# An attention and layer-norm kernel on one core: the last pairs' order written anew, and GpSimd's closing multiply and add of two tiles set apart

## The chip, the cores and the metric

The kernel runs on one core of a Trainium2 chip. TensorE (PE) multiplies, with its weight loads (PEld) beside it; VectorE (DVE), ScalarE (ACT) and GpSimd (POOL) work on tiles of 128 partitions; SyncE (SP) only issues transfers. ScalarE and GpSimd issue some transfers too. Each engine takes its instructions in the order in which they are written, and waits on semaphores where an input is not there yet. The metric is the time of one execution in microseconds (us), here the median of some runs.

## The reference

Cross-attention of 4 x 2048 rows of x (512 wide, 16 heads of 32) to 77 rows of context, a mask on the context, an output product, the residual and a layer norm with a scale and a shift:

```python
qs = (q @ wq).reshape(Bq, Lq, H, HD).transpose(0, 2, 1, 3)
ks_ = (k @ wk)...; vs = (v @ wv)...
scores = jnp.einsum('bhqd,bhkd->bhqk', qs, ks_) / jnp.sqrt(jnp.float32(HD))
scores = jnp.where(mask[:, None, :, :], -jnp.inf, scores)
attn_w = jax.nn.softmax(scores, axis=-1)
attn = jnp.einsum('bhqk,bhkd->bhqd', attn_w, vs)
out = attn.transpose(0, 2, 1, 3).reshape(Bq, Lq, H * HD) @ wo + q
mu = jnp.mean(out, axis=-1, keepdims=True)
var = jnp.mean((out - mu) ** 2, axis=-1, keepdims=True)
return (out - mu) / jnp.sqrt(var + EPS) * gamma + beta
```

All is float32. gamma and beta are drawn, not ones and zeros.

## The kernel before

The 8192 rows are 64 tiles of 128 (t = 0 to 63), two tiles make a pair (b = 0 to 31), four a group (16 groups). A float32 product is done as three products of parts: each operand is split into a high part and a low rest, and high x high, high x low and low x high are added up.

No loop and no planner sets the order. A string, ORDER, lists some 2,100 words, one for each step, in the order in which they are written to the engines; a table at the end of the kernel maps the first letter to a function. The number is a tile, pair or group, the figure behind the point a quarter or a part. The words of the stretch that changes, by engine:

- TensorE: Q60 (one quarter of a group's queries, 12 products), S58 (a tile's scores, 64 small products), V26 (a pair's weights times values, 32), O48 (a tile's output product, 12), X62 (x itself as the first product of an output). W62 and W63 are V for single tiles of the last pair.
- VectorE: q (queries out of PSUM), T58.2 (mask and maxima of four heads), r (reciprocal of the sums), t (transpose of the weights), b and d (the low part of V's and W's result), + and $ (the residual, into SBUF or kept in PSUM), s (mean and variance), y and z (subtract the mean and multiply by gamma; multiply by the inverse root and add beta), >63.0 and >63.1 (z for tile 63 in halves), h (r for a half tile).
- ScalarE: e58.2 (exponentials of four heads), a and c (the high part of V's and W's result), i (high part of x), k and % (scale and shift of a tile), = (mean and variance of tiles 60 and 62 there).
- GpSimd: n and m (the weights times the reciprocals), j (low part of x), v and u (inverse roots for a pair, for one tile), @ (u and the shift), f (times gamma, plus beta: two operations on 128 x 512).
- Transfers: x (a tile of x in), w and < (a result out, < in halves) from SyncE, the last half from ScalarE; P26.4s (part 4 of 12 of pair 26's regrouped weights, from SyncE; a: from ScalarE, g: from GpSimd), U62.5g the same for a single tile of the last pair; g (x transposed, for the queries).

So a tile ends in one of two ways: by s, u, y, z on VectorE, or by s, @ or v, % or k, and f on GpSimd; then w stores it. V reads what all 12 P of its pair have brought; t needs n, n needs r, r needs four e, and each e its T.

Two tables go with ORDER. SLOTS gives, for each buffer, the slot that it takes in the order of allocation; "mm" are the eight banks of PSUM, and whoever takes a bank waits until its last holder has been read. PADS gives for each Q and O (in base 36) how many empty instructions stand between its 12 products.

The functions of this change and of the prediction: rsqrt_one (L640, inverse root), shift_one (L648), centre and finish (L656, L661, L664 for the halves), stats_act (L634), affine (L619 to L622), store and store_half (L624, L670), regroup_part (L487, transfers at L493), o_proj (L568, products at L579), av_tile (W, products at L522).

Of the kernel before, what the change touches and what calls it, by code (L numbers as in the profile page):

```python
# [131 lines left out]
P28.10g x55 P28.2g x61 S61 P28.4g e60.1 +53 P28.6g O51 r59 T60.3 n59 k47 T61.2 e60.3 T61.0 T61.3 f47 S62 T61.1
e60.0 t59 V27 e61.1 r60 T62.2 e61.3 P29.11s P29.0g T62.3 O52 P29.7g x50 s51 P29.4g P29.8s a27.0 T62.0 P29.3g a27.1
P29.2s s53 P29.6g e61.0 w45 P29.1g V28 b27.0 P29.10s n60 y51 e61.2 x62 b27.1 T62.1 O55 a28.0 r61 @53 a28.1 $50
e62.3 +52 n61 b28.1 b28.0 k46 S63 t60 e62.2 x54 f46 O54 e62.1 t61 P29.5a +55 w46 e62.0 T63.1 X63 P30.11g P29.9s
T63.0 P30.5g O57 P30.6s P30.3g T63.2 e63.1 P30.1s u51 r62 s52 P30.0s n62 e63.2 s50 P30.2s P30.8s X62 T63.3 e63.3
P30.10s s55 V29 u50 w47 y50 e63.0 @52 z51 @55 z50 w51 O56 a29.0 h63.0 P30.4a $57 m63.0 h63.1 a29.1 b29.0 P30.9a s57
m63.1 P30.7a b29.1 O58 %55 u57 t62 %53 f55 %52 $56 U62.2s U62.11a V30 $54 U62.1s U62.10a +58 U62.6s U62.3a f53 t63
U62.4a O59 a30.0 a30.1 s58 U63.4s U63.1a U63.11s b30.0 @58 U62.8a U62.9s b30.1 U62.0a s56 U62.7s O61 U63.9a U62.5g
# [39 lines left out]
def xattn_layernorm(  # L179
# [410 lines left out]
    def residual_psum(t):  # L590
        nc.vector.tensor_tensor(pos[t], pos[t], od[t], ALU.add)
# [27 lines left out]
    def affine(t):  # L619
        o = od[t]  # L620
        nc.gpsimd.tensor_tensor(o, o, gam, ALU.mult)  # L621
        nc.gpsimd.tensor_tensor(o, o, bet, ALU.add)  # L622
# [11 lines left out]
    def stats_act(t):  # L634
        mv = mvs[t, 1] = tiny.tile([P, 4], F32, tag="mvt", bufs=64 - LATE, name=f"mvt_{t}")
        nc.scalar.activation(od[t], pos[t], AF.Copy, scale=-1.0 / D, accum_out=mv[:, 3:4])
        nc.scalar.activation(od[t], pos[t], AF.Square, bias=mv[:, 3:4], accum_out=mv[:, 1:2])
# [196 lines left out]
```

## Time and profile before

| | us |
|---|---|
| median of 3 runs (lowest, highest) | 510.38 (510.31, 512.49) |
| the profiled execution's own time | 509.93 |
| its span | 508.1 |
| TensorE busy | 497.6 |
| VectorE busy | 471.3 |
| ScalarE busy | 465.6 |
| GpSimd busy | 420.0 |

The profile is of one execution. Its times count from the start of the span. A row of the timeline has the start, the length, the engine, the line and what is written and read, and in brackets how long the engine stood idle before it and for whom. "x4" means four instructions in a row. Lengths overlap a little at their ends, since an engine begins the next while it drains the last; the step from start to start is then the better measure.

### The profile page before, as it was taken

The page shows a single profiled execution, that of the slowest core. Times are in us where ns is not written, and L with a number is a line of the kernel's source. Part 1 is how long each engine was busy: PE and PEld are TensorE (multiplying, and loading weights), DVE is VectorE, ACT ScalarE, POOL GpSimd, SP SyncE. Part 2 cuts the span into 40 slices and gives each one's busy share as a digit, 9 for nine tenths or more (in the row PEclk, how much of TensorE's full clock was granted, in tenths as well). Part 3 has the DMA queues.
Part 4 walks back from the last instruction along what each step waited for, and adds up shares of the span by engine and source line. Part 5 has one row for each costly group of instructions (what it writes and reads, how often), then busy time and mean ns, then how long its engine had stood idle before and what let it go on. Part 6 is the DMA issues. An engine that isn't in the chain of part 4 may idle for free.

```text
span 508.1 us, 21810 instructions
## 1 busy us (share of the span) xinstructions
PE 497.6 (98%) x6834; PEld 384.0 (76%) x6834; DVE 471.3 (93%) x2565; ACT 465.6 (92%) x2228; POOL 420.0 (83%) x388
## 2 busy tenths in 40 slices
PE   8999999999999999999999999999999999999994
PEld 6987777777777777777777877777787777776663
DVE  5798999999999999999999999999999999999986
ACT  6699999998999999999999999999999999999622
POOL 2573756999978998989899898888989679999986
PEclk9999999999999999999999999999999999999999
DMA  8947767878987687796877678777777687777755
GB/s 298 397 154 215 177 185 171 239 195 237 261 239 220 192 243 198 204 261 189 237 205 239 198 218 229 213 226 211 225 207 219 182 225 214 209 210 198 213 153 228
DMA packets 59236, 110.96 MB, mean 218 GB/s; under 512 B 9430, under 2 KB 12270, under 8 KB 59126
## 3 DMA queue, kind: packets, MB, share of 16 engines
q1 hardware_dynamic: 54854, 101.63, 69.1%
q0 software_dynamic: 2624, 6.16, 4.4%
q10 hardware_dynamic: 1648, 1.77, 1.4%
q8 instruction: 60, 0.98, 0.9%
q14 instruction: 50, 0.41, 0.3%
HBM read 41.79 MB, written 16.78 MB: 115 GB/s over the span
## 4 chain that ended last, share of the span: by engine, by line
PE 85%; DVE 5%; DMA 4%; POOL 3%; SPq 2%; issue 1%; ACTq 0%; ACT 0%; DVEq 0%
PE pq L290 33%; PE po L579 28%; PE sc L414 10%; PE pa L507 10%; PE pv L341 2%; DVE pbuf L431 1%; DVE B L482 1%; PE pk L313 1%; DMA xtl<-x 1%; DMA PT<-B 1%; SPq L493 1%; DMA first_xth<-xw 1%; POOL mvt L646 1%; PE pq L724 1%; DVE q L304 0%
## 5 line engine op out<-in xcount | busy, mean ns | idle before, releaser
L446 ACT ACTIVATE pbuf<-pbuf,nm 128x77 f32<-128x77 f32 x1024 | 352.4, 350 | 3.6 <-DVE nm L431 3.4
L446 ACT ACTIVATION_READ_ACCUMULATOR pbuf<-pbuf,nm 128x1 f32 x1024 | 195.3, 191 | 0.0
L431 DVE CUSTOM_DVE_ANT_0 pbuf<-sc,mb 128x77 f32<-128x77 f32 x1024 | 170.8, 232 | 6.8 <-PE sc L414 3.6
L461 POOL TENSOR_TENSOR pbuf<-pbuf,ri 128x1232 f32<-128x1232 f32 x63 | 142.8, 2268 | 29.1 <-DVE ri L456 27.6
L579 PE MATMUL po<-woh,AH 128*128 128x512 f32 x256 | 102.1, 399 | 0.4 <-DVE nm L431 0.4
L290 PE MATMUL pq<-xth,wqh 128*128 128x512 f32 (+1 forms) x256 | 101.2, 395 | 0.3
L579 PE MATMUL po<-woh,AL 128*128 128x512 f32 x256 | 99.8, 390 | 0.8 <-DVE AL L540 0.8
L579 PE MATMUL po<-wol,AH 128*128 128x512 f32 x256 | 99.7, 390 | 0.0
L290 PE MATMUL pq<-xth,wql 128*128 128x512 f32 (+1 forms) x256 | 98.1, 383 | 0.0
L290 PE MATMUL pq<-xtl,wqh 128*128 128x512 f32 (+1 forms) x256 | 98.1, 383 | 0.0
L482 DVE STREAM_TRANSPOSE B<-pbuf 128x1280 f32<-128x1280 f32 x64 | 96.1, 1501 | 0.9 <-POOL pbuf L461 0.2
L431 DVE DVE_READ_ACCUMULATOR2_ANT nm<- 128x1 f32 x1024 | 83.8, 82 | 0.0
L273 POOL TENSOR_TENSOR xtl<-xtf,xth 128x1024 fp32r<-128x1024 f32 x28 | 67.3, 2406 | 4.3 <-ACT xth L269 4.3
L622 POOL TENSOR_TENSOR o<-o,bet 128x512 f32<-128x512 f32 x51 | 66.0, 1294 | 4.0
L414 PEld LDWEIGHTS sc<-kct,q 32*64 32x64 f32 x4096 | 51.2, 130 | 22.2 <-issue 11.0
L621 POOL TENSOR_TENSOR o<-o,gam 128x512 f32<-128x512 f32 x51 | 67.0, 1314 | 0.2 <-issue 0.2
L414 PE MATMUL sc<-kct,q 32*64 32x77 f32 x4096 | 60.6, 238 | 0.0
L507 PE MATMUL pa<-PT,vsb 96*32 96x256 f32 x992 | 59.7, 382 | 0.0
L579 PEld LDWEIGHTS po<-woh,AH 128*128 128x128 f32 x256 | 48.0, 188 | 13.9 <-issue 1.7
L290 PEld LDWEIGHTS pq<-xth,wqh 128*128 128x128 f32 x256 | 48.1, 188 | 12.3 <-issue 1.2
L579 PEld LDWEIGHTS po<-woh,AL 128*128 128x128 f32 x256 | 48.1, 188 | 11.6 <-DVE AL L540 1.5
L290 PEld LDWEIGHTS pq<-xth,wql 128*128 128x128 f32 x256 | 48.1, 188 | 9.7
(127 smaller groups left out, 641.9 us busy)
## 6 DMA issues: line engine op xcount, KB each, us to landing
PT<-B SPq DMA_DIRECT2D x337, 128.0 KB
xtf<-xT SPq DMA_DIRECT2D x28, 512.0 KB
o<-x SPq DMA_DIRECT2D x56, 256.0 KB
out<-o SPq DMA_DIRECT2D x56, 256.0 KB
PT<-B POOLq DMA_DIRECT2D x29, 128.0 KB, 3.9
stage_a<-wk SPq DMA_DIRECT2D x4, 256.0 KB
stage_b<-wo SPq DMA_DIRECT2D x4, 256.0 KB
stage_a<-xT SPq DMA_DIRECT2D x2, 512.0 KB
```

The lines of the kernel that those rows point to most:

```text
L273: nc.gpsimd.tensor_tensor(l[:, c : c + 2], fx.pop((g, c)), xh[g][:, c : c + 2].bitcast(F32), ALU.subtract)
L290: nc.tensor.matmul(pq, w[:, c, m * P : (m + 1) * P], r[g][:, c, rs], start=(n == 0), stop=(n == 11))
L341: nc.tensor.matmul(pv[: rows.stop - rows.start], ctx_s[c][i][:, rows], v[c], start=(n == 0), stop=(n == 11))
L414: mm = nc.tensor.matmul(sc[j][r0 : r0 + SR, g * NK : (g + 1) * NK], qs[q, g, rs.start + r0 : rs.start + r0 + SR], kct[q, g, t // TPB, keys ...
L431: nc.vector.tensor_tensor_reduce(pb[:, h // 2, (h % 2) * NK : (h % 2 + 1) * NK], scs[t][j][:, g * NK : (g + 1) * NK], mb[:, t % TPB, keys_ ...
L446: nc.scalar.activation(pb[:, h // 2, (h % 2) * NK : (h % 2 + 1) * NK], pb[:, h // 2, (h % 2) * NK : (h % 2 + 1) * NK], AF.Exp, bias=nmax[t ...
L461: nc.gpsimd.tensor_tensor(pv, pv, rv.to_broadcast((P, NP, 2, NK)), ALU.mult)
L482: nc.vector.transpose(bt.rearrange("p c q r -> p q c r"), pbuf[t % NPB].rearrange("p q (c r) -> p q c r", c=5),)
L507: nc.tensor.matmul(pas[b, g // 2][HD * j : HD * (j + 1), (g % 2) * BLK : (g % 2 + 1) * BLK], vsb[:, 2 * b // TPB, h % 2, HD * (h // 2) : H ...
L579: nc.tensor.matmul(pos[t], a[:, c, rs], w[:, c, :], start=(first and c == 0 and n == 0), stop=(c == NC_D - 1 and n == 2),)
L621: nc.gpsimd.tensor_tensor(o, o, gam, ALU.mult)
L622: nc.gpsimd.tensor_tensor(o, o, bet, ALU.add)
```

## The change

`affine` gets an argument for one of its two operations, and two new words call it: [58 and [61 multiply by gamma, ]58 and ]61 add beta. f58 and f61 go. On GpSimd the end reads

```
before: f52 @61 u56 u59 f58 u60 f61 u62 u63
after:  f52 [58 @61 u56 u59 ]58 u60 [61 u62 u63 ]61
```

From the middle of pair 24 on (word 1,619 of some 2,100) the words of all engines are in another order, the same words otherwise. With it go the slots of "mm" and "o" from there, and the pads: 4 instead of 0 for Q56 to O48 and Q60 to Q62, 12 for Q63, one or two more or less in some visits before.

```diff
@@ -117,29 +117,29 @@
 P23.7s r48 w38 +43 i28 n48 P23.2s s43 k40 P23.4s S50 +42 e49.2 w41 V22 j28 T50.1 P23.10s T50.0 P23.6s e50.1 T50.2
 P23.1s S51 s42 x46 a22.0 P23.0s e49.1 T50.3 Q54 v21 P23.3s t48 P23.9s f40 k43 P23.11s T51.0 P23.8s a22.1 Q55 e50.2
 T51.2 P23.5s r49 g30 b22.1 x49 n49 e50.3 b22.0 T51.3 T51.1 O45 e50.0 q55 f43 t49 e51.0 q54 P24.7s O44 e51.3 r50 w40
-+45 n50 P24.4s s45 e51.2 P24.3s P24.9s S52 i29 +44 x63 P24.2g M60.4 P24.11s V23 e51.1 T52.2 P24.1g P24.5s j29 T52.0
-P24.6s e52.2 T52.3 S53 P24.0s t50 x51 e52.3 Q56 P24.8s r51 T52.1 n51 a23.0 T53.0 e52.1 s44 Q58 q56 a23.1 v22 e52.0
-T53.2 b23.0 b23.1 P24.10a t51 S54 k44 e53.0 O46 r52 P25.3g P25.7s T54.1 n52 g31 T53.3 e53.2 P25.6s T53.1 w43 T54.0
-e53.1 Q59 P25.2s T54.3 f44 x60 T54.2 e53.3 P25.11s t52 P25.5s e54.0 P25.9s S55 M56.4 P25.1s r53 +46 Q57 n53 e54.1
-q59 P25.10s T55.0 P25.0s e54.3 T55.2 P25.8s q58 P25.4g V24 e54.2 q57 t53 a24.0 S56 i30 T55.1 P26.10g P26.2s r54
-a24.1 O47 x56 T56.0 j30 e55.2 x57 b24.0 x48 b24.1 P26.0s e55.0 s46 P26.5s T55.3 O49 P26.11g w44 e55.3 T56.3 P26.4g
-P26.3s +47 n54 P26.8s T56.2 e55.1 P26.1s T56.1 V25 $49 e56.0 r55 t54 n55 e56.2 S57 x52 s49 O48 x58 i31 T57.3 u49
-y49 k42 j31 s47 e56.3 T57.0 Q60 T57.2 e57.3 f42 t55 a25.0 P26.7a z49 P27.7s Q61 e56.1 $48 w42 q60 P26.6g w49 T57.1
-e57.2 P27.11g P26.9s s48 P27.1g S58 P27.3g e57.0 q61 x53 P27.2g y48 Q63 P27.4s u48 r56 a25.1 T58.2 n56 k45 T58.3
-e57.1 b25.0 T58.0 Q62 T58.1 e58.0 P27.8g z48 P27.10g r57 w48 b25.1 e58.1 n57 t56 P27.5s S59 P27.6s e58.2 V26 q62
-f45 T59.2 e58.3 t57 O50 a26.0 a26.1 T59.1 P28.11s e59.2 P27.0g T59.0 P28.1s P28.7g q63 P27.9s e59.0 v23 r58 S60
-b26.0 P28.9s T59.3 P28.8s X51 e59.1 n58 b26.1 P28.5s T60.1 O53 x59 T60.0 e59.3 P28.3s T60.2 P28.0s t58 e60.2
-P28.10g x55 P28.2g x61 S61 P28.4g e60.1 +53 P28.6g O51 r59 T60.3 n59 k47 T61.2 e60.3 T61.0 T61.3 f47 S62 T61.1
-e60.0 t59 V27 e61.1 r60 T62.2 e61.3 P29.11s P29.0g T62.3 O52 P29.7g x50 s51 P29.4g P29.8s a27.0 T62.0 P29.3g a27.1
-P29.2s s53 P29.6g e61.0 w45 P29.1g V28 b27.0 P29.10s n60 y51 e61.2 x62 b27.1 T62.1 O55 a28.0 r61 @53 a28.1 $50
-e62.3 +52 n61 b28.1 b28.0 k46 S63 t60 e62.2 x54 f46 O54 e62.1 t61 P29.5a +55 w46 e62.0 T63.1 X63 P30.11g P29.9s
-T63.0 P30.5g O57 P30.6s P30.3g T63.2 e63.1 P30.1s u51 r62 s52 P30.0s n62 e63.2 s50 P30.2s P30.8s X62 T63.3 e63.3
-P30.10s s55 V29 u50 w47 y50 e63.0 @52 z51 @55 z50 w51 O56 a29.0 h63.0 P30.4a $57 m63.0 h63.1 a29.1 b29.0 P30.9a s57
-m63.1 P30.7a b29.1 O58 %55 u57 t62 %53 f55 %52 $56 U62.2s U62.11a V30 $54 U62.1s U62.10a +58 U62.6s U62.3a f53 t63
-U62.4a O59 a30.0 a30.1 s58 U63.4s U63.1a U63.11s b30.0 @58 U62.8a U62.9s b30.1 U62.0a s56 U62.7s O61 U63.9a U62.5g
-y57 U63.10g U63.3a s54 U63.6g U63.0s U63.5a U63.7g U63.2s y54 U63.8a u54 w50 O60 +61 %58 f52 w53 z54 s61 $59 y56
-W62 @61 s59 W63 c62 u56 z57 u59 c63 d62 O62 $60 f58 y59 =60 d63 z59 %61 y60 O63 w59 u60 =62 z56 w58 f61 z60 w57 y62
-w56 w60 s63 w52 w55 u62 y63 w61 u63 z62 w54 w62 >63.0 <63.0 >63.1 <63.1
++45 n50 P24.4s s45 i29 w43 P24.5s e51.2 S52 +44 P24.11s P24.1g M60.4 P24.3s V23 e51.1 T52.1 j29 P24.6s T52.2 P24.0s
+e52.2 T52.3 S53 P24.9s t50 P24.8s a23.1 Q56 a23.0 e52.3 r51 T53.2 n51 T52.0 P24.10a s44 Q58 e52.1 b23.0 v22 T53.0
+e53.0 q56 b23.1 P24.2g t51 S54 e52.0 O46 q58 P25.1s e53.2 M56.4 x51 T53.3 P25.6s k44 r52 T53.1 P25.7s n52 e53.3 Q59
+T54.3 x48 T54.0 P25.5s e53.1 T54.2 P25.10s t52 g31 P25.3g e54.0 P25.0s P25.4g S55 P25.9s r53 T54.1 Q57 n53 P25.8s
+i30 T55.0 x63 e54.3 +46 P25.2s T55.2 P25.11s f44 T55.3 e54.2 V24 q57 q59 e54.1 t53 S56 j30 a24.0 T55.1 a24.1 O47
+P26.1s e55.1 b24.0 x56 b24.1 P26.0s T56.0 e55.0 P26.9s P26.10g r54 T56.2 n54 O49 T56.3 e55.2 T56.1 +47 e55.3 s46
+P26.11g S57 P26.4g $49 e56.0 r55 V25 t54 n55 P26.7a i31 s49 O48 e56.1 T57.3 u49 y49 j31 t55 a25.1 a25.0 Q61 k42 s47
+P27.5s e56.3 f42 x61 z49 P27.9s T57.0 e57.3 P26.8s T57.2 Q60 P26.3s q61 e56.2 P26.5s b25.0 P27.11g T57.1 P26.2s
+P26.6g k45 $48 P27.6s P27.8g r56 e57.0 S58 w49 s48 P27.10g w44 P27.1g q60 Q62 P27.3g e57.2 T58.3 P27.2g y48 n56
+e57.1 T58.1 T58.0 Q63 T58.2 e58.1 x53 u48 r57 b25.1 n57 z48 e58.2 t56 w48 V26 x58 e58.0 P27.4s q62 P27.0g P27.7s
+t57 e58.3 f45 S59 x62 O50 a26.1 T59.2 e59.2 T59.0 T59.1 v23 w45 a26.0 q63 P28.5s e59.1 T59.3 S60 x55 r58 P28.11s
+P28.10g b26.0 e59.0 n58 b26.1 O53 w42 T60.2 P28.9s T60.0 e59.3 x50 T60.1 x54 P28.0s t58 X51 e60.2 P28.2g P28.3s
+P28.6g S61 P28.4g P28.1s k47 +53 P28.7g P28.8s O51 r59 e60.0 T60.3 n59 x52 T61.1 e60.1 T61.3 T61.0 f47 S62 T61.2
+e60.3 t59 V27 e61.1 r60 T62.1 n60 a27.0 P29.2s T62.3 O52 e61.3 P29.8s s51 x57 T62.0 e61.2 x59 T62.2 P29.7g P29.11s
+b27.0 P29.6g V28 w47 a27.1 P29.3g $50 P29.10s e61.0 P29.0g s53 P29.9s P29.1g b27.1 P29.4g O55 a28.0 r61 @53 a28.1
+y51 P29.5a b28.0 n61 k46 b28.1 +52 e62.3 S63 t60 f46 e62.2 O54 t61 e62.0 T63.0 u51 w46 e62.1 T63.1 X63 P30.2s T63.2
+P30.11g P30.8s O57 e63.1 +55 P30.3g P30.0s P30.5g r62 T63.3 P30.6s n62 e63.3 s50 P30.1s x60 s55 V29 e63.2 s52 u50
+y50 e63.0 @55 O56 z51 @52 z50 w51 P30.9a P30.10s h63.0 $57 a29.0 m63.0 h63.1 a29.1 s57 P30.4a X62 m63.1 b29.0
+P30.7a b29.1 O58 %55 u57 t62 %52 f55 %53 $56 U62.2s U62.3a $54 V30 U62.6s U62.10a +58 U62.1s U62.4a f53 t63 U62.11a
+O59 a30.0 a30.1 s58 U63.0s U63.3a U62.7s b30.0 @58 U63.1a U63.11s s56 U62.0a U62.9s y57 U63.8a U63.10g b30.1 O61
+U63.6g U62.8a s54 U62.5g U63.4s U63.9a U63.7g U63.2s y54 U63.5a u54 O60 $59 %58 f52 y56 +61 s61 z54 W62 [58 z57 W63
+c62 s59 w57 @61 w55 c63 d62 O62 w53 u56 $60 w52 d63 u59 =60 ]58 y60 y59 %61 O63 u60 w58 z59 =62 z56 [61 w59 z60 w56
+y62 w50 u62 w54 s63 w60 z62 u63 y63 w62 ]61 >63.0 <63.0 >63.1 <63.1 w61
 """
 
 SLOTS = {
@@ -147,8 +147,8 @@
         "7012346570123574602317546023417520135467205130427631724352760134217346516034572160435170425361024713"
         "4627016534270452736107245320164735206147265310742635102347560123745627104365270143205617342065172643"
         "5071263450231746052371462750136427051320465731206457261340752631402357160423751627405361270453201647"
-        "3520614726531074263510234756012374562710436527014320561734206517264350712654032057104627510423564107"
-        "5632376435735164203615724016547605160451764057164236436460"
+        "3520614726531074263510234756012374562710436527014320561734206517264350712635034720135604275104236751"
+        "4203467142562174035074632140736471067341073610743257457476"
     ),
     "q": "1010101010101010",
     "xth": "010101010101010101",
@@ -158,7 +158,7 @@
     "B": "0101011010101010101010101010101010",
     "AH": "1010010101010101010101010101010101",
     "AL": "1010010101010101010101010101010101",
-    "o": "765401237654231607541237510462375104623751046237510462375160714",
+    "o": "765401237654231607541237510462375104623751046237510462375176140",
     "nm": "0120102101201201201201201201201201201201201201201201201201201201",
     "sum": "0120102101201201201201201201201201201201201201201201201201201201",
     "ri": "0120120120120120120120120120120120120120120120120120120120120120",
@@ -170,8 +170,8 @@
 }
 
 PADS = (
-    "f8680000000000000000000686000cddlmmllllllllmmmmmmmmmmmmmmmmmmmmikkkkkkkkkkkkkkkkkkkkkkkkkkkkkkjkkk00"
-    "000000000000000000000000"
+    "f8680000000000000000000686000cddlmmlllllmmmmmmmmmmmmmmmmmmmmmmkkkkkkkkkkkkkkkkkkkkkkkkkkkkkkmmlmmm44"
+    "444444444c00000000000000"
 )
 
 
@@ -616,10 +616,10 @@
         rn = rns[t // 2]
         nc.scalar.activation(o, o, AF.Identity, bias=rn[:, 1, tt : tt + 1], scale=rn[:, 0, tt : tt + 1])
 
-    def affine(t):
+    def affine(t, n=None):
         o = od[t]
-        nc.gpsimd.tensor_tensor(o, o, gam, ALU.mult)
-        nc.gpsimd.tensor_tensor(o, o, bet, ALU.add)
+        for i in (0, 1) if n is None else (n,):
+            nc.gpsimd.tensor_tensor(o, o, (gam, bet)[i], (ALU.mult, ALU.add)[i])
 
     def store(t):
         nc.sync.dma_start(out[t * P : (t + 1) * P, :], od.pop(t))
@@ -769,6 +769,7 @@
         "w": lambda k, part: store(k), "*": lambda k, part: hold(k), "#": lambda k, part: residual_late(k),
         "&": lambda k, part: split_hi(k, nc.scalar), "~": lambda k, part: split_lo(k),
         "=": lambda k, part: stats_act(k), ">": finish_half, "<": store_half,
+        "[": lambda k, part: affine(k, 0), "]": lambda k, part: affine(k, 1),
         "$": lambda k, part: residual_psum(k),
         "@": lambda k, part: (rsqrt_one(k), shift_one(k)), "%": lambda k, part: scale_one(k),
     }
```

## The prediction

> **What bounds the kernel now.** I read the page first: span, then the chain that ended last.
>
> ```profile
> span 508.1 us, 21810 instructions
> ```
> ```profile
> PE 85%; DVE 5%; DMA 4%; POOL 3%; SPq 2%; issue 1%; ACTq 0%; ACT 0%; DVEq 0%
> ```
>
> TensorE carries 85% of the chain. So the second view is the busy time by stretch, cut at the first changed word (about 392 us) and at TensorE's last product but three (columns: stretch, length, then busy time and instructions of PE, PEld, DVE, ACT, POOL, then clock, DMA share, GB/s):
>
> ```profile
> 392.00:491.50 99.50, 99.14 (x1331) 73.25 (x1330) 96.46 (x497) 88.02 (x440) 86.90 (x99) 1.00 0.75 205
> ```
>
> TensorE is busy 99.14 of 99.50 us. The waits view for the end of the run shows the gap:
>
> ```profile
> PE po L579 <- DVE nm L431: 0.4, 1, 0.4
> ```
>
> That one wait is all there is to gain on TensorE before 491.5. The time that the change can move lies behind it, so I read that stretch engine by engine. TensorE first:
>
> ```profile
> 491.31 0.39 PE L579 MATMUL po<-wol,AH 128*128 128x512 f32 x1
> 491.54 0.39 PE L579 MATMUL po<-woh,AL 128*128 128x512 f32 x1
> 491.86 1.08 PE L522 MATMUL pa<-PT,vsb 96*32 96x128 f32 x32
> 493.40 1.08 PE L522 MATMUL pa<-PT,vsb 96*32 96x128 f32 x32 [0.47 <-DVE po L591]
> 494.41 0.50 PE L579 MATMUL po<-woh,AH 128*128 128x512 f32 x1
> 494.75 0.40 PE L579 MATMUL po<-wol,AH 128*128 128x512 f32 x1
> 495.92 0.50 PE L579 MATMUL po<-woh,AL 128*128 128x512 f32 x1 [0.78 <-DVE AL L540]
> ```
>
> These are O60's end, W62, W63 and O62's first three products. Two waits: 0.5 us ahead of W63, and, between O62's second and third product (0.23 us apart when nothing waits), 0.94 us for VectorE's d62. VectorE itself stood still shortly before:
>
> ```profile
> 488.10 0.76 DVE L659 SCALAR_TENSOR_TENSOR po<-po,mvt,gam 128x512 f32<-128x512 f32 x1
> 489.24 0.69 DVE L588 TENSOR_TENSOR xtl<-po,xtl 128x512 f32<-128x512 f32 x1 [0.38 <-PE po L579]
> 491.01 0.75 DVE L662 SCALAR_TENSOR_TENSOR o<-po,mvt,bet 128x512 f32<-128x512 f32 x1 [1.07 <-POOL mvt L646]
> ```
> ```profile
> 495.19 0.68 DVE L540 TENSOR_TENSOR AL<-pa,AH 128x512 fp32r<-128x512 f32 x1
> 495.78 0.69 DVE L591 TENSOR_TENSOR po<-po,xtl 128x512 f32<-128x512 f32 x1
> ```
> ```profile
> 499.89 0.75 DVE L662 SCALAR_TENSOR_TENSOR xtl<-po,mvt,bet 128x512 f32<-128x512 f32 x1 [0.19 <-POOL mvt L646]
> 500.56 0.75 DVE L659 SCALAR_TENSOR_TENSOR po<-po,mvt,gam 128x512 f32<-128x512 f32 x1
> 501.24 0.70 DVE L630 BATCH_NORM_STATS2 st<-po 128x6 f32<-128x512 f32 x1
> ```
> ```profile
> 503.40 0.75 DVE L662 SCALAR_TENSOR_TENSOR xtl<-po,mvt,bet 128x512 f32<-128x512 f32 x1 [0.46 <-POOL mvt L646]
> 504.19 0.87 DVE L666 SCALAR_TENSOR_TENSOR xtl<-po,mvt,bet 128x256 f32<-128x256 f32 x2
> ```
>
> In words of the order: y54, +61, z54; d62, $60; z60, y62, s63; z62 and the two halves >63. VectorE waits 0.38 for O61, 1.07 for u54, 0.19 for u60 and 0.46 for u62. The last store then leaves from ScalarE's queue, and the span ends 3.0 us after its issue:
>
> ```profile
> 505.10 0.36 ACTq L672 DMA_DIRECT2D out<-xtl  x1
> ```
>
> **The change, part by part.** Sums are made against the profiled execution (span 508.1, time 509.93); the median shown is 510.38, 0.45 above it.
>
> *The fill on VectorE before d62.* After y54 (end 488.86) the old queue has +61 z54 s61 $59 y56 s59 z57 d62, the new one $59 y56 +61 s61 z54 z57 s59 d62: the same seven, but $59 and y56, whose inputs are older, stand where the engine waited. From 488.86 to d62 at 495.19 are 6.33 us, less 0.38 and 1.07 idle 4.88 of work: d62 can start at 493.74. Its input is c62 on ScalarE, 493.06 plus 0.59:
>
> ```profile
> 493.06 0.59 ACT L536 CAST AH<-pa 128x512 fp32r<-128x512 f32 x1 [3.51 <-PE pa L522]
> ```
>
> That is 493.65, so d62 runs 493.74 to 494.42, 1.45 earlier. Bounds: 0 if something else holds VectorE, 1.45 if nothing does. I take 1.45: the seven are known.
>
> *GpSimd's four transfers and W62, W63.* The old order issues U62.5g, U63.10g, U63.6g, U63.7g:
>
> ```profile
> 487.91 2.21 POOL L493 DMA_DIRECT2D PT<-B  x4 [0.59 <-DMA PT<-B]
> ```
> ```profile
> DMA to landing us min/median/max: 3.7/3.8/3.9
> ```
>
> So U62.5g lands at 487.91 + 3.8 = 491.7, just ahead of W62 at 491.86, and the fourth, issued at about 489.6, lands near 493.2, which fits W63 at 493.40 (the name L591 beside that wait had no product for it). The new order puts U62.5g third, 2 x 0.55 later. Two things pay for that. First, n60 now stands ahead of the six P29 transfers, where GpSimd waited:
>
> ```profile
> 456.12 1.28 POOL L622 TENSOR_TENSOR o<-o,bet 128x512 f32<-128x512 f32 x1
> 458.37 3.21 POOL L493 DMA_DIRECT2D PT<-B  x6 [0.97 <-DVE nm L431]
> ```
>
> GpSimd gains up to 0.97 there (bounds 0 and 0.97; I take 0.9), so U62.5g is issued at 487.91 - 0.9 + 1.1 = 488.1. Second, the old queue of SyncE issues stores 50 and 53 just ahead of these transfers:
>
> ```profile
> 487.70 1.09 SPq L625 DMA_DIRECT2D out<-o  x2
> ```
> ```profile
> 488.00:490.00 2.00, 2.00 (x11) 1.65 (x10) 1.52 (x3) 0.82 (x1) 2.00 (x4) 1.00 0.92 263
> ```
>
> The DMA share is 0.92 while they are written. In the new queue both stand behind w57, which needs z57, the sixth of the seven VectorE operations above, so they leave after 492. An earlier transfer of GpSimd's, one of pair 25 with no store beside it, landed sooner:
>
> ```profile
> DMA to landing us min/median/max: 2.5/2.5/2.5
> ```
>
> Between 2.5 and 3.8 I take 2.7, nearer the row without stores: U62.5g lands at 490.8, U63.7g by 491.4, both ahead of W62, whose start stays (O60 ends as before, and W62 follows its last product by 0.32 in any case). W63 follows W62 after 1.01 (493.40 to 494.41 is that step): 492.87. O62 starts at 493.88, its second product 0.34 and its third 0.57 later, at 494.45; with d62 ready at 494.42 that is 494.47 in place of 495.92: TensorE ends **1.45 us earlier**, 499.8 for the start of s63's input in place of 501.24. At 3.8 the landing is 491.9 and W62 slips by 0.1.
>
> [...]
>
> *VectorE behind d62.* Again the same operations in another order: $60 d63 y60 y59 z59 z56 z60 y62 s63 z62 y63 >63 >63. Old: from 495.19 to the end of >63.1 at 504.19 + 0.87 = 505.06 are 9.87 us, 0.65 of them the two waits for u60 and u62: 9.2 of work. New: y60 moves up to third place and needs both passes of =60, which wait for $60:
>
> ```profile
> 496.50 0.60 ACT L636 ACTIVATE xtl<-po 128x512 f32<-128x512 f32 x1 [1.38 <-DVE po L591]
> ```
> ```profile
> 497.81 0.19 ACT L637 ACTIVATION_READ_ACCUMULATOR xtl<-po,mvt 128x1 f32 x1
> ```
>
> =60 begins as $60 ends (495.78 + 0.69) and takes 1.50. New: $60 at 494.33 to 495.02, =60 to 496.52, while VectorE is through with d63 at 495.5: a **new wait of 1.0 us**. This is what the reorder costs. End: 493.74 + 9.2 + 1.0 = 503.95, against 505.06: 1.1 earlier. s63 comes at 493.74 + (501.24 - 495.19 - 0.19) + 1.0 = 500.6, behind O63's end, so TensorE no longer sets the end: VectorE does.
>
> *The split on GpSimd.* Old: f52, @61 u56 u59, f58, u60, f61, u62, u63. New: the halves stand apart.
>
> ```profile
> 493.54 0.19 POOL L645 TENSOR_TENSOR mvt<-mvt,small 128x1 f32<-128x1 f32 x1
> ```
> ```profile
> 496.26 1.30 POOL L621 TENSOR_TENSOR xth<-xth,gam 128x512 f32<-128x512 f32 x1
> ```
>
> @61, u56 and u59 take 493.54 to 496.26, 2.72; each half 1.3, a u some 0.8. f52, 0.9 earlier, ends at 492.7; [58 to 494.0, the three to 496.75, ]58 to 498.1, u60 to 498.9, [61 to 500.2, u62 to 501.1, u63 after s63 (500.6 + 0.9) to 502.3, ]61 to 503.6. z60 (needed at 499.2) and z62 (501.5) find theirs ready by 0.3 or more; whole f61 ahead of u62 would have made z62 wait 0.9. The work is the same; what it costs is that ]61 and its store come last: w61 leaves at 503.65 with the half <63.1 (503.98), twice its bytes. The transfers' rate at the end, when they are full, is 406 GB/s:
>
> ```profile
> 502.00:504.00 2.00, 0.00 (x0) 0.00 (x0) 1.51 (x3) 0.00 (x0) 1.75 (x5) 1.00 1.05 406
> ```
>
> As an estimate from it 256 KB take 0.65 us, so w61 delays the last landing by 0 to 0.65; I take 0.2, since the stores that crowded this row leave from 492 on.
>
> *The rest of the reorder (392 to 491).* TensorE's words are the same with the same number of products; six words change places with a neighbour (S57 and V25, Q60 and Q61, Q62 and Q63, S59 and V26, X51 and O53, X62 behind V29 and O56). On GpSimd's queue P24.2g moves behind j29, n51 and v22, on SyncE's w43 moves ahead of P24.5s, w51 ahead of P30.10s, and the loads x48 to x63 change places: the same transfers, covered by the time between a part's landing and its product (the view of waits names no transfer for TensorE's products there). If that cover is gone, TensorE waits one for one. The bank of O47 now comes from q59 instead of T55.1, which may save the 0.4 wait; but VectorE, 96.46 of 99.50, is as full and gates the tail as above, so I take 0, bounds -0.4 to +1.0 (the second rival). Pads: the products of wol wait for nothing in any of their 256 places, with 0 pads as with 22, so 4 cost nothing:
>
> ```profile
> L579 PE MATMUL po<-wol,AH 128*128 128x512 f32 x256 | 99.7, 390 | 0.0
> ```
>
> **Sum**: -1.1 + 0.2 = -0.9, from 509.93 to 509.0; against the median, 509.5.
>
> **Rivals.** *Only part of it comes.* If VectorE is held at +61 or s59 as before, or the transfers still land at 3.8 and more because other stores have taken that place, d62 moves by 0.5 instead of 1.45 while y60's wait stays: 493.74 + 0.95 brings the end to 504.9, and the last store of 256 KB takes it back: -0.1 to +0.3, 510.3 to 510.7. For: no gap in VectorE's fill to spare (0.09 us between c62 and d62). Against: the seven's inputs are all older.
>
> *Slower: V26 waits for its data.* SyncE's new queue puts P27.5s, which needs t55, ahead of P26.8s, P26.3s, P26.5s and P26.2s; V26 also moves ahead of S59, so it is due about 0.9 before its old start:
>
> ```profile
> 429.76 1.51 DVE L482 STREAM_TRANSPOSE B<-pbuf 128x1280 f32<-128x1280 f32 x1
> ```
> ```profile
> 441.92 0.85 PE L507 MATMUL pa<-PT,vsb 96*32 96x256 f32 x12
> ```
> ```profile
> 462.30 6.36 DMA xtl<-x
> ```
>
> If t55 ends at 431.27 as before, P26.2s is the seventh issue behind it, at 431.3 + 6 x 0.6 = 434.9; with the longest landing the chain shows, 6.36, it is there at 441.3, 0.3 after V26's new place at 441.0. t55 now stands ahead of s47 and two groups of maxima, some 2 us, so the margin is 1.8. It decides once t55 is over 2.7 late, or other transfers in the queue stretch by as much in all: then TensorE, with no slack, passes on each us. At 2.5 past the point the time is 509.5 + 2.5 = 512.0.
>
> *The change does not do what it says:* u62 and u63 come earlier and nobody waits less, for s63 and TensorE hold the end: then z62 ahead of y63 saves the 0.46 and w61 at the end costs it: 510.2 to 510.5.
>
> **How the numbers follow.** Forecast (-0.4 to -1.6, 508.8 to 510.0) 0.52; the first and third rival together 0.28; the slower one and other stalls of its kind 0.18, of it a third beyond 512.9; a larger gain 0.02. Half a per cent, 2.55 us, is about what a measurement can tell from no change; all that waits behind 491.5 is less, so faster by that has 0.03, slower 0.07, the same 0.90. The range 508.5 to 511.6 takes in the first three and the near half of the stalls.
>
> **What would show it.** Right: d62 near 493.8 and no wait between O62's products; W63 1.0 after W62; VectorE idle 1 us ahead of y60 for =60; POOL's transfers near 487 to 489 with no store beside; the end with w61. Wrong: waits on TensorE between 392 and 491, V26 or V30 first (P30.10s now stands behind w51); VectorE idle elsewhere behind 488; W62 later than O60's end.

## The result and the profile after

The changed kernel is slower: 514.09 us median of 6 runs (513.19 to 515.52), beside 510.64 (6 runs) for the kernel before on the same chip; the ratio is 1.0061, 95% interval 1.0039 to 1.0083. The forecast was 509.5, its range ended at 511.6. The profiled execution of the kernel after is the longest of its six (515.52), so its parts below add up to more than the 3.45 between the medians.

The span, the stretch view (cut 0.89 later than for the kernel before, which is what the kernel after lags by at that point; columns as there) and TensorE's waits of the kernel after:

```profile
span 513.7 us, 21893 instructions
```
```profile
392.89:497.52 104.63, 101.21 (x1331) 75.34 (x1330) 100.11 (x500) 88.56 (x440) 88.22 (x100) 0.98 0.72 191
```
```profile
PE pa L507 <- DMA PT<-B: 1.8, 1, 1.8
PE sc L414 <- DVE nm L431: 1.6, 2, 1.3
```

The same 1,331 products take 104.63 us in place of 99.50. TensorE is idle for 3.42 instead of 0.36, and busy 2.07 longer, at a granted clock (the share of TensorE's full clock that the chip allowed it) of 0.98 instead of 1.00. Both waits lie between 392 and 491, where the prediction had put a zero. TensorE's rows of the kernel after show the first of them:

```profile
398.62 0.35 PE L414 MATMUL sc<-kct,q 32*64 32x77 f32 x4
400.24 0.31 PE L414 MATMUL sc<-kct,q 32*64 32x77 f32 x2 [1.27 <-DVE nm L431]
400.87 1.35 PE L414 MATMUL sc<-kct,q 32*64 32x77 f32 x58 [0.32 <-DVE nm L431]
402.16 0.80 PE L290 MATMUL pq<-xth,wqh 128*128 128x512 f32 x1
402.75 0.63 PE L290 MATMUL pq<-xtl,wqh 128*128 128x512 f32 x1
...
405.59 0.39 PE L290 MATMUL pq<-xth,wql 128*128 128x512 f32 x1
```

and the same words in the kernel before:

```profile
397.72 0.96 PE L414 MATMUL sc<-kct,q 32*64 32x77 f32 x64
398.61 0.50 PE L290 MATMUL pq<-xth,wqh 128*128 128x512 f32 x1
398.95 0.40 PE L290 MATMUL pq<-xtl,wqh 128*128 128x512 f32 x1
...
401.22 0.39 PE L290 MATMUL pq<-xth,wql 128*128 128x512 f32 x1
```

These are S53 and the first two and the last of Q56's twelve products. From S53's start to Q56's are 3.54 us in place of 0.89: 2.65 more, 1.59 of it the two waits and 1.06 products that come in pieces or run slower. Q56's first two products then stand 0.59 apart instead of 0.34, and its last begins 3.43 behind its first instead of 2.61: 0.8 more. Over both the granted clock (last column but two) is down:

```profile
398.00:400.00 2.00, 0.97 (x20) 0.32 (x8) 2.00 (x8) 0.43 (x3) 1.24 (x1) 1.00 0.84 249
400.00:402.00 2.00, 1.44 (x60) 1.34 (x60) 2.00 (x19) 1.66 (x9) 0.00 (x0) 0.62 0.79 184
402.00:404.00 2.00, 2.00 (x16) 1.52 (x6) 1.99 (x15) 2.00 (x10) 1.00 (x1) 0.53 0.30 67
```

What S53 waits for is VectorE's maxima of tile 52 (L431), and these stand behind one conversion of the mask, M60.4. The rows of M60.4 (VectorE), of j29 (GpSimd) and of i29 (ScalarE, whose result j29 reads) in the kernel before:

```profile
395.69 0.35 DVE L397 TENSOR_SCALAR mb<-m 128x384 bf16<-128x384 uint8 x1
...
396.46 2.40 POOL L273 TENSOR_TENSOR xtl<-xtf,xth 128x1024 fp32r<-128x1024 f32 x1
...
395.09 1.03 ACT L269 CAST xth<-xtf 128x1024 fp32r<-128x1024 f32 x1
```

and in the kernel after:

```profile
396.59 2.87 DVE L397 TENSOR_SCALAR mb<-m 128x384 bf16<-128x384 uint8 x1
...
396.86 2.37 POOL L273 TENSOR_TENSOR xtl<-xtf,xth 128x1024 fp32r<-128x1024 f32 x1
...
394.63 1.04 ACT L269 CAST xth<-xtf 128x1024 fp32r<-128x1024 f32 x1
```

The same operation on the same 128 x 384 bytes takes 2.87 us in place of 0.35, and ends at 399.46, 0.23 behind j29.

The second wait is V28's, for parts of pair 28. SyncE begins to issue the last of them 10.4 us ahead of V28's start in the kernel before (450.5 against 460.92), and 7.0 us ahead of the moment when V28 is due in the kernel after (458.0 against 465.0). The profile gives no landing time for SyncE's transfers, but for GpSimd's of the same line (L493) it does: those issued in 444 to 453 of the kernel before, then those in 455 to 459 of the kernel after, parts of pair 28 among them:

```profile
DMA to landing us min/median/max: 2.8/4.0/5.3
```
```profile
DMA to landing us min/median/max: 6.7/6.9/7.2
```

In the kernel after x55, w42, x50 and x54, 256 KB each, stand between V28's parts on SyncE's queue (before, x59 alone); around there the DMA share is 0.91, against 0.67 in the corresponding 20 us before:

```profile
440.00:460.00 20.00, 20.00 (x372) 14.21 (x372) 19.95 (x137) 20.00 (x108) 17.93 (x21) 1.00 0.67 178
```
```profile
444.00:464.00 20.00, 20.00 (x373) 14.21 (x372) 19.95 (x136) 19.62 (x107) 18.40 (x19) 1.00 0.91 234
```

The tail did what was forecast, except for its last store. Rows of the kernel after, TensorE, then VectorE (d62, y60 with y59, the halves of tile 63), then SyncE's last issue (w61):

```profile
497.88 1.95 PE L522 MATMUL pa<-PT,vsb 96*32 96x128 f32 x64
499.76 0.50 PE L579 MATMUL po<-woh,AH 128*128 128x512 f32 x1
500.10 0.40 PE L579 MATMUL po<-wol,AH 128*128 128x512 f32 x1
500.44 0.50 PE L579 MATMUL po<-woh,AL 128*128 128x512 f32 x1
```
```profile
499.71 0.68 DVE L540 TENSOR_TENSOR AL<-pa,AH 128x512 fp32r<-128x512 f32 x1
...
502.56 1.42 DVE L659 SCALAR_TENSOR_TENSOR po<-po,mvt,gam 128x512 f32<-128x512 f32 x2 [0.98 <-ACT xtl L637]
...
509.04 0.88 DVE L666 SCALAR_TENSOR_TENSOR xtl<-po,mvt,bet 128x256 f32<-128x256 f32 x2
```
```profile
509.97 0.38 SPq L625 DMA_DIRECT2D out<-xtl  x1
```

W62 and W63 run together, O62's third product follows the second by 0.34, and the new wait for =60 is 0.98. From W62's start to VectorE's end are 12.04 us (509.92 less 497.88) in place of 13.20 (505.06 less 491.86): 1.16 won. But the span ends 3.78 behind VectorE's end; before it was 3.04.

### The profile page after: what moved, and what is told of

Its sections match the earlier page's. It is cut to its first block, busy times and chain, and to the rows that moved or that the text cites. A ratio compares the mean times of both kernels' runs of the same rounds, so it can differ in the third digit from the quotient of the medians.

```text
span 513.7 us, 21893 instructions
## 1 busy us (share of the span) xinstructions
PE 500.2 (97%) x6834; PEld 386.1 (75%) x6834; DVE 476.1 (93%) x2565; ACT 465.8 (91%) x2228; POOL 419.2 (82%) x388
## 4 chain that ended last, share of the span: by engine, by line
PE 90%; DVE 6%; DMA 2%; ACT 0%; issue 0%; DVEq 0%
PE pq L290 33%; PE po L579 31%; PE sc L414 11%; PE pa L507 11%; PE pv L341 2%; PE pk L313 1%; DVE pbuf L431 1%; PE pq L724 1%; DMA PT<-B 1%; DVE po L659 1%; DVE st L630 1%; DMA first_xtl<-xw 1%; DVE mb L397 1%; PE po L566 1%; DVE xth L662 0%; DVE wvlAH L370 0%
## 5 line engine op out<-in xcount | busy, mean ns | idle before, releaser
L431 DVE CUSTOM_DVE_ANT_0 pbuf<-sc,mb 128x77 f32<-128x77 f32 x1024 | 170.9, 232 | 7.7 <-PE sc L414 4.6
L431 DVE DVE_READ_ACCUMULATOR2_ANT nm<- 128x1 f32 x1024 | 84.5, 82 | 0.0
L414 PE MATMUL sc<-kct,q 32*64 32x77 f32 x4096 | 61.8, 239 | 1.9 <-DVE nm L431 1.6
```

The costliest lines, as they stand in the source:

```text
L414: mm = nc.tensor.matmul(sc[j][r0 : r0 + SR, g * NK : (g + 1) * NK], qs[q, g, rs.start + r0 : rs.start + r0 + SR], kct[q, g, t // TPB, keys ...
L431: nc.vector.tensor_tensor_reduce(pb[:, h // 2, (h % 2) * NK : (h % 2 + 1) * NK], scs[t][j][:, g * NK : (g + 1) * NK], mb[:, t % TPB, keys_ ...
```

## The experiments

Every kernel below is compared with the kernel before on its own chip, whose median was 510.3 to 510.6 throughout; the bracket behind a ratio is its 95% interval. Words are shown as they stand in ORDER, and "..." stands for words left out.

**P24.2g put back.** In the kernel after GpSimd issues one transfer less ahead of j29, which looked like the reason that j29 got so near to M60.4.

```diff
-P24.1g ... b23.1 P24.2g
+P24.2g P24.1g ... b23.1
```

> The kernel after, with one word put back: P24.2g ahead of P24.1g on GpSimd. My theory: M60.4, VectorE's mask conversion (2.87 us in the kernel after, 0.35 before), is held until GpSimd's j29 ends, and it lies beside j29 only because P24.2g no longer stands ahead of it. Then j29 starts some 0.55 us later, M60.4 is back at 0.7 us or less, TensorE's two waits for VectorE's maxima (1.27 and 0.32 us) go, Q56 takes 2.9 us again, and the time falls by 3 to 3.9 us, to 510.2 to 511.1 with V28's wait left. Rival: TensorE's waits come from the new order of VectorE's maxima (T52.1 ahead of T52.2) and from the banks that S53 now takes from them, and M60.4's length is covered: then the waits stay and the time is within 0.5 us of 514.1.

Measured: 514.98 us (514.14 to 515.96), ratio 1.0087 [1.0069, 1.0105]. The expectation failed. The waits for the maxima stayed, as the rival had it, at 0.9 above the 514.1 that it named; and M60.4 got longer.

```profile
395.81 3.38 DVE L397 TENSOR_SCALAR mb<-m 128x384 bf16<-128x384 uint8 x1
...
396.59 2.37 POOL L273 TENSOR_TENSOR xtl<-xtf,xth 128x1024 fp32r<-128x1024 f32 x1
```

j29 now begins 0.78 us behind M60.4's start, as in the kernel before (0.77), and M60.4 is still held to j29's end (399.19 against 398.96). The distance is not the cause; that M60.4 ends with j29 is borne out, since it grew by the 0.5 that j29 was put off.

**Pair 28's parts ahead of the loads.**

```diff
-P28.5s x55 P28.11s w42 P28.9s x50 x54 P28.0s P28.3s P28.1s P28.8s x52
+P28.5s P28.11s P28.9s P28.0s P28.3s P28.1s P28.8s x55 w42 x50 x54 x52
```

> The kernel after, with the seven parts of pair 28 that SyncE issues standing together ahead of x55, w42, x50 and x54. My theory: V28's wait of 1.8 us comes from four 256 KB transfers ahead of these parts in the same queue; the last part is then issued some 3 us earlier and lands some 3 us earlier, V28 waits for nothing, and the time falls by 1.5 to 1.9 us from 514.1, to 512.2 to 512.6. Rival: all engines' transfers together fill the DMAs in 450 to 472 us (share 1.05), so that an earlier issue only moves the wait to GpSimd's parts of pair 28 (landing at 463), to pair 29's or to a residual load: then V28 or V29 still waits 0.5 us or more and the time falls by less than 1.0.

Measured: 512.77 us (512.23 to 514.53), ratio 1.0050 [1.0030, 1.0069]. V28 waits for nothing, as expected, and the median is 1.3 lower, between the two expectations; since the interval overlaps that of the kernel after, a gain is not shown by the times.

**Both.**

> Both edits in one kernel. If the two places are all that was lost, both gains add up to 5.0 to 5.7 us and only the tail's gain and O47's 0.4 are left of the change: 508.6 to 509.4, 1.2 to 2 under the kernel before. If the order between 392 and 491 loses elsewhere too (a wait that the first two had hidden), it is 510 or more.

Measured: 514.02 us (512.45 to 516.66), ratio 1.0076 [1.0049, 1.0103]. M60.4 is still held (3.38 us) and V28 waits for nothing, so this says nothing on the sum of the two gains; the median is 1.0 lower than with P24.2g alone, within the intervals.

**The new tail alone, on the kernel before** (the words from U62.2s on, with the split).

> The kernel before up to U62.2s, and from there the words of the kernel after (the tail with the split; slots and pads as before). By the prediction's steps VectorE's fill, the new wait of y60 and the split give -0.9: 509.7 against 510.6. By the trace of the kernel after (TensorE's lead of 1.48 at O63, the new wait of 1.0 on VectorE) -0.9 to -1.3. Rival: the tail gives nothing of its own, since VectorE's work and the last stores set the end: within 0.3 of the kernel before.

Measured: 510.34 us (12 runs, 509.79 to 511.46), ratio 0.9998 [0.9987, 1.0009]: nothing, where 0.9 was forecast. Its W62, last half and last store:

```profile
492.88 1.95 PE L522 MATMUL pa<-PT,vsb 96*32 96x128 f32 x64
...
504.28 0.88 DVE L666 SCALAR_TENSOR_TENSOR xtl<-po,mvt,bet 128x256 f32<-128x256 f32 x2
...
505.22 0.38 SPq L625 DMA_DIRECT2D out<-xtl  x1
```
```profile
span 509.1 us, 21811 instructions
```

VectorE ends 12.28 behind W62's start (505.16 less 492.88), 0.92 earlier than before, but the span ends 3.94 behind VectorE, 0.90 later: w61, 256 KB from SyncE, is issued last. The profile gives no landing time for it, but the span ends 3.9 behind its issue, where it ended 3.0 behind that of the last half before. In these traces the tail's gain is there on VectorE, and what follows w61's issue takes it back.

**M60.4 out of j29's way.** This asks whether M60.4 is the operation at fault at all, or the maxima behind it.

```diff
-+44 P24.11s P24.1g M60.4 ... t50 ... r51
++44 P24.11s P24.1g ... t50 M60.4 ... r51
```

> The kernel after, with M60.4 behind t50, where GpSimd has ended j29 and waits for r51. Putting P24.2g back did not shorten M60.4 (3.38 us, from 0.78 us ahead of j29 to 0.23 behind its end), so the distance to j29 was not it. Theory A: M60.4 is what can't go on beside j29; out of its way it takes 0.35 us, T52.1 follows +44 at once, TensorE's waits for VectorE's maxima (1.2 and 0.3 us) and Q56's slow start go, and the time falls by 2.5 to 3.9 us, to 510.2 to 511.6. Theory B: it is T52.1, the word behind it, that is held until j29 ends, and M60.4's row only covers the time: then +44 or T52.1 shows the same 2.5 us and the time stays within 0.5 of 514.1.

Measured: 510.60 us (10 runs, 509.5 to 512.18), ratio 0.9995 [0.9982, 1.0008]. M60.4 takes 0.32 us and S53 waits for nothing: 3.5 us less than the kernel after, by a move of one word whose result is not read before tile 60, with i29 still early. Theory A holds.

**The same with pair 28's parts ahead of the loads.**

> The same, and pair 28's parts from SyncE ahead of the four stores and loads (which alone gave 512.8 and no wait for V28). Theory A: both gains add up, 512.8 less 2.5 to 3.9 us: 508.9 to 510.3, as fast as the kernel before or up to 1.6 us faster. Theory B: 512.5 to 513.

Measured: 510.44 us (12 runs, 508.75 to 513.49), ratio 1.0003 [0.9986, 1.0019]. Just above the range expected (508.9 to 510.3), and no better than without the second edit.

**T52.1 and T52.2 exchanged, in the kernel after.**

> The kernel after, T52.1 and T52.2 exchanged, so that T52.2 follows M60.4 as in the kernel before; GpSimd's queue as in the kernel after (j29 0.27 us behind M60.4's start). Theory C: what follows M60.4 on VectorE decides whether M60.4 gets through ahead of j29; M60.4 takes 0.35 us. Theory A (distance to j29 alone decides): M60.4 takes 2.9 us as in the kernel after.

Measured: one run, 515.92 us. M60.4 takes 2.92 us, from 396.33 to 0.23 behind j29's end: theory C falls.

**P24.2g moved, in the kernel before.**

> The kernel before, with P24.2g behind v22 on GpSimd as in the kernel after, VectorE's order untouched; j29 begins some 0.2 us behind M60.4's start in place of 0.77. If the distance to j29 decides, M60.4 takes 2.6 us and the time is 2 to 3 us above the kernel before; if VectorE's own order decides, M60.4 takes 0.35 us and the time is that of the kernel before within 1 us.

Measured: one run, 510.73 us; M60.4 takes 0.35. Here j29 begins 0.52 behind M60.4 instead of the 0.2 that was meant, since it waits for its input; but with 0.78 between them M60.4 was held above, and with 0.52 it is not. So neither the word behind M60.4 nor the distance alone decides. The row of j29 shows what was left to look at:

```profile
395.39 0.35 DVE L397 TENSOR_SCALAR mb<-m 128x384 bf16<-128x384 uint8 x1
...
395.91 2.37 POOL L273 TENSOR_TENSOR xtl<-xtf,xth 128x1024 fp32r<-128x1024 f32 x1 [0.31 <-ACT xth L269]
```

j29 waits for ScalarE's i29. In the kernels so far where M60.4 stands ahead of j29 and is short, i29 ends some 0.4 us behind M60.4's start (before: 395.09 + 1.03 = 396.12 against 395.69); in each where it is held, i29 ended 0.9 ahead of it (after: 394.63 + 1.04 = 395.67 against 396.59). The diff moves i29: from behind e51.2 and S52 to ahead of e51.2.

**i29 put back, in the kernel after.**

```diff
-s45 i29 w43 P24.5s e51.2 S52 +44
+s45 w43 P24.5s e51.2 S52 i29 +44
```

> The kernel after, with one ScalarE word, i29, put back behind e51.2 and S52. New theory (D): GpSimd takes hold of the path that M60.4 needs as soon as j29's input is there and the operations before it are through, even while it still issues transfers; j29's input is i29's result. Where i29 ends 0.9 us ahead of M60.4's start (kernel after and three variants), M60.4 is held until 0.22 us behind j29's end; where i29 ends 0.42 us behind it (kernel before and two variants), M60.4 takes 0.35 us. With i29 back, M60.4 takes 0.35 us, TensorE has no wait for S53, and the time is that of the kernel with M60.4 moved, 510.1 to 511.1. Rival: another word of the new order makes the difference; then M60.4 takes 2.9 us and the time stays at 514.

Measured: 509.87 us (12 runs, 509.19 to 511.81), ratio 0.9991 [0.9980, 1.0002].

```profile
395.33 0.35 DVE L397 TENSOR_SCALAR mb<-m 128x384 bf16<-128x384 uint8 x1
...
395.92 2.37 POOL L273 TENSOR_TENSOR xtl<-xtf,xth 128x1024 fp32r<-128x1024 f32 x1 [0.39 <-ACT xth L269]
```

**i29 moved, in the kernel before.**

```diff
-s45 e51.2 P24.3s P24.9s S52 i29 +44
+s45 i29 e51.2 P24.3s P24.9s S52 +44
```

> The kernel before, with i29 alone moved to where the kernel after has it, behind s45 and ahead of e51.2. Theory D: M60.4 starts before j29 as it did, but is held until 0.22 us behind j29's end: 3.2 to 3.5 us in place of 0.35, T52.2 and what follows come 3 us later, and the time rises by 2 to 3.5 us, to 512.6 to 514.1. Rival: M60.4 stays at 0.35 us and the time within 0.5 of 510.6.

Measured: 514.11 us (4 runs, 512.79 to 516.19), ratio 1.0074 [1.0051, 1.0096].

```profile
396.14 3.33 DVE L397 TENSOR_SCALAR mb<-m 128x384 bf16<-128x384 uint8 x1
...
396.87 2.37 POOL L273 TENSOR_TENSOR xtl<-xtf,xth 128x1024 fp32r<-128x1024 f32 x1
...
394.17 1.04 ACT L269 CAST xth<-xtf 128x1024 fp32r<-128x1024 f32 x1
```

One word of ScalarE's, moved alone, makes a loss of the whole size in the kernel before (+3.8 us) and undoes it in the kernel after: 0.5 below the kernel before in place of 3.5 above it.

**M60.4 one word earlier.** Who gets through, M60.4 or the operation of GpSimd?

```diff
-+44 P24.11s P24.1g M60.4
+M60.4 +44 P24.11s P24.1g
```

> The kernel after, with M60.4 one word earlier on VectorE, ahead of +44, where VectorE stood idle for 0.7 us; i29, j29 and GpSimd's queue untouched. M60.4 then starts beside GpSimd's n50 instead of 0.36 us behind its end. Theory D (whoever asks first gets the path when the operation on GpSimd ends): M60.4 asks before j29 is next, and ends some 0.22 us behind n50, as the regular ones do behind their n: 0.7 to 1.2 us long; +44 comes 0.3 to 0.5 late, and TensorE's wait for S53 is gone: 510.3 to 511.1. Rival (a GpSimd operation whose input is there always goes first): M60.4 is held over n50 and j29, some 3.9 us, and the time is 514 or more.

Measured: one run, 510.57 us. The rows of M60.4, n50 and j29:

```profile
394.51 1.25 DVE L397 TENSOR_SCALAR mb<-m 128x384 bf16<-128x384 uint8 x1
...
393.30 2.26 POOL L461 TENSOR_TENSOR pbuf<-pbuf,ri 128x1232 f32<-128x1232 f32 x1
...
396.18 2.38 POOL L273 TENSOR_TENSOR xtl<-xtf,xth 128x1024 fp32r<-128x1024 f32 x1
```

M60.4 starts inside n50 and ends 0.20 behind n50's end (395.76 against 395.56), before j29, although i29 ends 0.56 ahead of n50's end as in the kernel after. It had started 0.49 ahead of i29's end (394.51 against 395.00). That agrees with theory D, by which whoever asks first gets through, and the rival (GpSimd always first) falls. One trace of this kernel is little, but the kernel before has the same eight times between 168 and 376 us: a conversion of the mask starts inside an n and ends 0.21 to 0.22 behind the n's end, while the f behind n on GpSimd takes 1.41 or 1.42 for its first operation in place of some 1.3. The first of the eight:

```profile
168.79 0.67 DVE L397 TENSOR_SCALAR mb<-m 128x384 bf16<-128x384 uint8 x1
...
166.98 2.27 POOL L461 TENSOR_TENSOR pbuf<-pbuf,ri 128x1232 f32<-128x1232 f32 x1
```

**i29 put back and pair 28's parts first.**

> The kernel after with i29 put back behind S52 and pair 28's parts from SyncE ahead of the four stores and loads. With i29 alone put back V28 still waited 0.6 us for its data; if that wait is on the path, the time falls by 0.6 more, to 509.3, 1.0 us under the kernel before (the tail's VectorE gain, less what store w61 at the end gives back, and O47's 0.4). If VectorE or the tail's stores set the end anyway, it stays at 509.9.

Measured: 510.00 us (13 runs, 509.45 to 513.07), ratio 0.9993 [0.9980, 1.0006]. V28's wait, which was 0.6 with i29 alone put back, is gone from the trace and worth nothing that can be measured:

```profile
PE pa L507 <- DMA PT<-B: 0.6, 1, 0.6
```

That is the row of V28 with i29 alone put back.

**The split alone, on the kernel before.**

> The kernel before with the split alone: [58 ahead of @61, ]58 in f58's place, [61 in f61's place, ]61 and store w61 behind u63 and z62. By the prediction: VectorE's wait of 0.46 us for u62 goes, w61 at the end costs 0.2: -0.3. By the trace of the kernel with the new tail (w61 lands 0.73 us behind the last half of tile 63): the store gives back all of it, +0.0 to +0.4. Both lie within 0.5 us of 510.6; the trace tells them apart by what lands last.

Measured: 510.32 us (12 runs, 509.86 to 511.5), ratio 1.0001 [0.9992, 1.0010]: no change; both readings of the expectation lie within what can be told from none. The trace sides with the second, which has the store give back the gain: VectorE ends 12.48 behind W62's start instead of 13.20 (504.18 less 491.70), and the span ends 4.0 behind VectorE instead of 3.0.

**The new tail without the split.** Contrary to the words of the expectation f61 stands in the place of ]61, behind u63, so that both of its operations come after the last inverse root. What the expectation asks, f61 whole ahead of u62, was not run.

> The kernel before with the new tail, but f58 and f61 whole (in the places of ]58 and [61), w61 behind z62. If the split is what the new tail needs, z62 waits some 0.9 us for u62 behind f61 and VectorE ends 0.9 us later than with the split, while w61 no longer lands last and gives back 0.7: 510.5 to 510.9 against 510.3 for the new tail with the split. If the split costs more than it brings, 509.6 to 510.0.

Measured: 511.79 us (12 runs, 510.99 to 512.82), ratio 1.0024 [1.0013, 1.0034]. VectorE's last halves and w61 in it:

```profile
503.95 0.88 DVE L666 SCALAR_TENSOR_TENSOR xtl<-po,mvt,bet 128x256 f32<-128x256 f32 x2
```
```profile
506.03 0.33 SPq L625 DMA_DIRECT2D out<-xtl  x1
```

VectorE is through at 504.83, and the last store leaves 1.20 later (0.06 with the split). So the end follows w61, which comes 1.1 later against VectorE's end, and having one operation instead of two behind u63 is worth some 1.4 us in this tail (ratios 1.0024 and 0.9998); the tail as a whole is worth nothing.

## Why the prediction was wrong

*The step that failed* is the one on "the rest of the reorder (392 to 491)", taken at 0 with bounds -0.4 to +1.0. It went through the moved words of TensorE, GpSimd and SyncE, looked for late transfers and banks, and left out ScalarE's and VectorE's. The loss sits there: i29, one word (e51.2, the exponentials of four heads) earlier on ScalarE, lets GpSimd's j29 stand ready before VectorE's M60.4 asks; M60.4 is then held for 2.5 us more, tile 52's maxima come late, S53 waits 1.59, and slower and scattered products make 3.5 us of it on TensorE (2.65 at S53, 0.8 more over Q56). Runs show it in both directions: i29 moved alone, +3.8 us; put back alone, 0.5 below the kernel before instead of 3.5 above. That it goes by way of M60.4 is shown by the kernel with M60.4 behind t50, where i29 is early and nothing is lost (510.60). What bore on it stood in the profile of the kernel before. M60.4 began 0.43 us ahead of i29's end, and the mask conversions of one shape took from 0.35 to 1.49 us, those above 0.35 from 138 us on each ending 0.21 to 0.23 behind an operation of GpSimd's (columns: start, length):

```profile
138.40 1.49 DVE L397 TENSOR_SCALAR mb<-m 128x384 bf16<-128x384 uint8 x1
...
395.69 0.35 DVE L397 TENSOR_SCALAR mb<-m 128x384 bf16<-128x384 uint8 x1
```

A spread of four times for one shape was a warning that was not read. "Covered by the time between a part's landing and its product" was an argument on transfers and could not see an operation that is held with no wait shown, as M60.4 was for 2.87 us.

*The slower rival* had the right sign and the right kind of place for the second wait: a V that waits for its data because SyncE's new queue puts other transfers ahead. It named V26, which waited for nothing; it was V28, two pairs later, 1.83 us in the trace. With M60.4 held, taking it away lowered the median by 1.3, within the intervals; with i29 back the wait was 0.6 and taking it away changed nothing (509.87 and 510.00). So that this wait cost time is not shown. The point at which the rival was to decide, t55 over 2.7 late, does not follow from the margin of 1.8 that it works out.

*VectorE's fill before d62* (1.45 earlier): right. From W62's start to O62's third product are 2.56 us in place of 4.06, 1.50 less.

*GpSimd's transfers*: right. The landing line of the four in the kernel after:

```profile
DMA to landing us min/median/max: 2.3/2.5/3.1
```

2.7 was taken for them, with no store beside, and W63 follows W62 at once. That the 3.8 of the trace before was the price of two stores beside them is argued from these rows (3.8 before, 2.5 here) and the stores' places.

*VectorE behind d62* (a new wait of 1.0, VectorE's end 1.1 earlier): right; 0.98 and 1.16 (0.92 in the tail alone). That VectorE sets the end was right for TensorE's part in it, but the span's end follows w61.

*The split and w61 last* (0.2 from an estimate between 0 and 0.65): a term of the right sign and mis-sized, outside its own bounds: 0.74 in the kernel after, 0.90 with the tail alone and 0.98 with the split alone. The estimate took the bytes at the full rate of 406 GB/s; in the traces the span ends 3.7 to 4.0 behind w61's issue, in the kernel before 3.0 behind that of the last half. With 0.9 in its place the sum for the tail is about -0.2 instead of -0.9, and the runs of the tail alone give -0.1 (-0.7 to +0.5), which leaves no room for the forecast.

*Pads and the moved words of TensorE*: right as far as can be told. With i29 back the whole of the new order between 392 and 491, pads too, costs nothing that can be measured, and the 0.4 that O47 waited for its bank is gone from the waits, as the lower bound had it.

So two steps failed: the zero for the reorder, which measured 3.5 to 3.8 by one word of ScalarE's and decides the result, and the size of the last store, which takes the tail's gain. All of the change but i29 gave 509.87, 0.5 below the kernel before (-1.0 to +0.1); the -0.9 forecast lies in that interval, but the tail from which it was added up does not bear it out. No kernel of these is faster than the kernel before by more than its interval.

## What to carry to other kernels

When a long list of instructions is reordered, walk every engine's list, and for each moved word ask whose input becomes ready earlier, not only whose becomes late: an operation that is ready sooner can hold one of another engine's: M60.4, 0.35 us alone, took 2.87, to 0.23 behind the end of j29's 2.37. Where the duration of one shape varies fourfold in a profile (0.35 to 1.49 us for the mask conversions), look for a neighbour whose end its own end follows; such an operation belongs where that neighbour waits, as M60.4 behind t50 (0.32 us there). And a last store of full size is better priced by the time from its issue to the span's end (3.7 to 4.0 us here, against 3.0 for a half) than by its bytes.

## What the runs showed of the hardware

**VectorE held with no wait shown.** The conversion from uint8 to bf16 in SBUF (0.35 us alone) ends 0.20 to 0.23 us behind the end of a GpSimd operation that holds it: 0.23 behind j29 in the kernel after, 0.23 with i29 moved alone (399.47 against 399.24), 0.20 behind n50 with M60.4 a word earlier, 0.21 to 0.22 behind eight n of the kernel before. The profile shows it as the operation's own length, with no wait: 2.87 us for M60.4 in the kernel after, and no idle time of VectorE's ahead of it. Why the one operation holds the other no run here shows. That the one that asks first goes first, as theory D has it, and that GpSimd's asks when its input is there, while it still issues transfers, and not at the start that its row shows (j29's lies 0.3 to 0.8 us behind that of the M60.4 that it holds), fits every kernel here in which M60.4 stands ahead of j29 (j29 holds it where i29 ends some 0.9 us ahead of M60.4's start, and not where i29 ends 0.4 to 0.5 behind it), but is argued from the starts and not seen itself.

**The clock behind short waits.** After 1.59 us of waits in which S53 came in pieces the granted clock was 0.62 and 0.53 in two stretches of 2 us; with i29 moved alone, after one wait of 1.9, it was

```profile
402.00:404.00 2.00, 2.00 (x6) 1.52 (x6) 2.00 (x17) 1.99 (x10) 1.00 (x1) 0.50 0.44 130
```

while V28's wait of 1.83, between long products, left it at 1.00 in each 2 us from 463 to 471. Why it was down after the one wait and not after the other no run here shows. Of the 3.5 us that the held conversion cost, 1.9 were not waiting but products that ran slower or in pieces.
